# Layer 0 attention from the third batch on: weighted sums kept with features on partitions, even and odd heads joined by small transfers in place of transposes

## The chip, the cores and the metric

The kernel runs on one core of a Trainium2 chip. The metric is device time in microseconds (us) of one execution. Inputs and outputs lie in HBM, and the whole two-layer network is one launch.

## The reference, cut to what matters

`x` and `ctx` are 8 batches of 256 tokens by 256 features, in float32. Two layers follow one another; each adds a gated attention and a gated feed-forward part to `x`. Only the attention of layer 0 is touched by the change:

```python
def _L0_xattn_ref(Q, K, V, Wq, bq, Wk, bk, Wv, bv, Wo, bo):   # 16 heads of 16 features
    q, k, v = Q @ Wq + bq, K @ Wk + bk, V @ Wv + bv           # each to (B, 16, S, 16)
    scores = jnp.einsum('bhqd,bhkd->bhqk', q, k) * scale
    attn = jax.nn.softmax(scores, axis=-1)
    out = jnp.einsum('bhqk,bhkd->bhqd', attn, v)
    out = out.transpose(0, 2, 1, 3).reshape(B, S, D_MODEL)
    return out @ Wo + bo
x = x + jnp.tanh(g_xattn[0]) * _L0_xattn_ref(_layernorm(x), ctx_1024, ctx_1024, ...)
x = x + jnp.tanh(g_ffn[0]) * _L0_ffn_ref(_layernorm(x), ...)                  # 64 slots, top 8, GRU
x = x + jnp.tanh(g_xattn[1]) * _L1_xattn_ref(ctx_1024, _layernorm(x), ...)    # 8 heads of 128
x = x + jnp.tanh(g_ffn[1]) * _L1_ffn_ref(_layernorm(x), ...)                  # fake-quantized SwiGLU
```

## The kernel before, in words

**Tiles and engines.** A batch is one tile of 128 partitions x 2 x 256. TensorE (PE) does matmuls and 128x128 transposes into PSUM; PSUM has four banks tagged `m`, three tagged `z` and one tagged `s`. Batches 0 and 1 of layer 0 run first, together with the preparation of the weights. Batches 2 to 7 of layer 0 and the slot feed-forward of layer 0 then run beside the attention of layer 1 (`attention1`), which goes through 8 batches x 8 heads. The feed-forward of layer 1 comes last.

**What sets the order.** `layer0()` makes a list of pieces for each batch, each piece with a cost. The lists of batches 2 to 7 are joined with the pieces of the slot sets (`merge`) into the queue `side`. For each head of layer 1, `attention1` spends a share of credits on pieces of this queue, half after the softmax of the head and half at the end of the step. The share is worked out from the costs that are left and from the heads at which a batch must be ready. Below that, a tile scheduler decides the order on each engine by when an instruction is ready in its own planning; each engine then runs strictly in that order, and so does the queue of DMAs on SyncE (SP).

**Layer 0 attention of one batch.** Sixteen heads are taken in four groups `g` of four heads (`HG = 4`).

- `value` (L556 to L573): `ve` holds, for 128 keys and each head, 16 columns of values and 16 columns of ones. Two additions on VectorE (DVE, L568) write the values.
- `stack` (L593 to L611): for batches from 2 on, queries and keys were split into a high and a low half and stored to a DRAM scratch, and two transfers (L601) and four transfers (L605) on SP bring four heads of a group into the tiles `k` and `q` of one of two pairs.
- `scores`, `maxima`, `exps` (L613 to L653): the matmuls of L623, a negated maximum on DVE (L626), its transpose (L636), and the matmuls of L649 with the exponential on ScalarE (ACT, L652).
- `sums` (L655 to L675): eight matmuls (L660), four heads side by side: rows 32j to 32j+15 of the bank are the weighted values of head j by feature, rows 32j+16 to 32j+31 are sixteen equal copies of its sum of exponentials. ACT copies the bank to `oS` (L675).
- `divide` (L677 to L692): two transposes of `oS` (L682) put tokens on partitions, DVE takes the reciprocal of the eight sums of a token (L685) and multiplies (L687) into `o`.
- `turn_o` (L694): when all four groups are done, four transposes (L272, called from `turned`) bring `o` back to features on partitions, and ACT copies them to `oT` (L696).
- `finish` (L698 to L710): four matmuls with `wo` (L703), and DVE adds the result to `x` with its gate (L710).

Layer 1's parts that appear below: `query` L1045 and L1054, `key` L1081 and L1088, `value` L1101 and L1108, scores L1124 with the maximum on DVE (L1125) and the exponential on ACT (L1126), L1127 and L1128 on DVE, `turn_e` L1138 with the copies L1142 (DVE) and L1144 (ACT), `sums` L1152, and the turn of the latents (L272, then L1035 on DVE).

In the trace a float32 matmul has two records, a transpose has one, and the matmuls of L623 and L649 have one.

Of the kernel before, what the change touches and what calls it, by code (L numbers as in the profile page):

```python
# [9 lines left out]
F32 = mybir.dt.float32  # L10
# [6 lines left out]
ALU = mybir.AluOpType  # L17
# [4 lines left out]
P = 128  # L22
B, S, D = 8, 256, 256
EPS = 1e-5
H0, DK0 = 16, 16
HG = 4
# [17 lines left out]
BASE, ZERO = 1024.0, 1152.0  # L44

WARM = (12, 8, 15, 9)

SLOT_SETS = ((0,), (1,), (2, 3), (4, 5), (6, 7))

# [51 lines left out]
def flamingo_kernel(ctx: ExitStack, tc: tile.TileContext, a: dict, out: bass.AP):  # L101
    nc = tc.nc
    V, A, G, T = nc.vector, nc.scalar, nc.gpsimd, nc.tensor
# [10 lines left out]
    def bank(tag, dtype=F32):  # L114
        return psum.tile([P, 512], dtype, tag=tag, name=f"bank_{tag}", bufs=BANKS[tag])
# [9 lines left out]
    def load_tokens(b, queue):  # L125
        queue.dma_start(out=xs[b], in_=x_in[b])
        queue.dma_start(out=cs[b], in_=c_in[b])

    def rows(pool, tag, ap, n, queue):

        t = pool.tile([P, n], F32, tag=tag, name=tag)
        queue.dma_start(out=t, in_=ap.partition_broadcast(P))
        return t
# [24 lines left out]
    at0 = right0.enter_context(tc.tile_pool(name="at0", bufs=2, side="right"))  # L158
# [16 lines left out]
    bv = rows(w0, "bv", a["L0_xattn_bv"], D, nc.sync)  # L175
# [293 lines left out]
    class Batch0:  # L469
# [86 lines left out]
        def value(self):  # L556
            pp = self.bank().rearrange("p (m t) -> p m t", m=2)
            for m in range(2):
                for c in range(2):
                    T.matmul(  # L560
                        pp[:, m, :],
                        self.cT[:, c, m * P : (m + 1) * P],
                        wv[:, c, :],
                        start=c == 0,
                        stop=c == 1,
                    )
            for m in range(2):
                V.tensor_tensor(  # L568
                    self.ve[:, m, :, :DK0],
                    pp[:, m, :].rearrange("p (h e) -> p h e", e=DK0),  # L570
                    bv.rearrange("p (h e) -> p h e", e=DK0),
                    ALU.add,
                )  # L573
# [19 lines left out]
        def stack(self, g):  # L593

            if self.b < 2:
                return self.spread(g)
            q, k = self.pairs[g % 2]
            at = slice(g * HG, (g + 1) * HG)
            for i in range(2):
                half = 2 * DK0 * i  # L600
                nc.sync.dma_start(  # L601
                    out=k[half : half + 2 * DK0, :, :].bitcast(F32), in_=self.dk[:, :, at, :]
                )
            for r in range(4):
                ins = nc.sync.dma_start(  # L605
                    out=q[r * DK0 : (r + 1) * DK0, :, :].bitcast(F32), in_=self.dq[r // 2][:, at, :]
                )
            for far in (1, 2):
                if g == far - 1 and (far == 2 or self.b == 2) and self.b + far < B:
                    with tc.issue_after(ins.ins):  # L610
                        load_tokens(self.b + far, nc.sync)  # L611
# [43 lines left out]
        def sums(self, g):  # L655

            po = self.bank()[:, :S]

            def product(kc, j):
                return T.matmul(  # L660
                    po[32 * j : 32 * j + 32, :],
                    self.ve[:, kc, g * HG + j, :],
                    self.e[j // 2][:, j % 2, kc, :],
                    start=kc == 0,
                    stop=kc == 1,
                ).ins


            with tc.issue_after(product(0, HG - 1)), tc.high_priority():
                for j in range(HG - 1):  # L670
                    product(0, j)
                for j in range(HG):
                    product(1, j)
            self.oS = self.pool.tile([P, S], F32, tag="oS", name="oS", bufs=1)
            A.copy(self.oS, po)  # L675

        def divide(self, g):  # L677
            if g == 0:
                self.o = self.tmp(name="o") if self.b == 0 else at0.tile([P, 2, D], F32, tag="o", name="o", bufs=1)
            pt = self.bank()[:, : 2 * P].rearrange("p (c t) -> p c t", c=2)  # L680
            for qc in range(2):
                T.transpose(pt[:, qc, :], self.oS[:, qc * P : (qc + 1) * P], ident)  # L682
            pv = pt.rearrange("p c (j e) -> p c j e", e=2 * DK0)
            rs = small.tile([P, 2, HG], F32, tag=f"rs0{self.s}", name="rs0")
            V.reciprocal(rs, pv[:, :, :, DK0])  # L685
            at = g * HG * DK0
            V.tensor_tensor(  # L687
                self.o[:, :, at : at + HG * DK0].rearrange("p c (h e) -> p c h e", e=DK0),
                pv[:, :, :, :DK0],
                rs[:, :, :, None].to_broadcast([P, 2, HG, DK0]),  # L690
                ALU.mult,
            )  # L692
# [19 lines left out]
    def layer0():  # L712


        bs = [Batch0(b) for b in range(B)]
        out = [[] for _ in range(B)]

        def piece(cost, obj, name, *args):
            return (cost, lambda: getattr(obj, name)(*args))

        def head(me, groups):
            return [
                piece(0.0, me, "norm"),
                piece(0.5, me, "turn_c"),
                piece(1.8, me, "key"),
                piece(0.5, me, "turn_x"),
                piece(1.8, me, "query"),
            ] + [piece(0.0, me, "stack", g) for g in groups]

        def maxima(me, g):  # L730
            return [piece(0.5, me, "scores", g, qc) for qc in range(2)] + [piece(0.1, me, "maxima", g)]

        for b in range(2):
            out[b] += head(bs[b], range(2)) + maxima(bs[b], 0)
        for b in range(B):
            me = bs[b]
            after = bs[b + 1] if 0 < b < B - 1 else None
            for g in range(NG):
                nxt = (me, g + 1) if g + 1 < NG else (after, 0)
                far = (me, g + 2) if g + 2 < NG else (after, g + 2 - NG)  # L740
                work = [piece(0.5, me, "exps", g, 0)]
                if nxt[0]:
                    work.append(piece(0.5, nxt[0], "scores", nxt[1], 0))
                work.append(piece(0.5, me, "exps", g, 1))
                if nxt[0]:
                    work.append(piece(0.5, nxt[0], "scores", nxt[1], 1))
                if g == 0:
                    work.append(piece(1.8, me, "value"))
                if after:
                    if g == 0:  # L750
                        work.append(piece(0.0, after, "norm"))
                    if g == 1:
                        work.append(piece(0.5, after, "turn_x"))
                        work.append(piece(0.5, after, "turn_c"))
                        work.append(piece(1.8, after, "query"))
                    if g == 2:
                        work.append(piece(1.8, after, "key"))
                if nxt[0]:
                    work.append(piece(0.1, nxt[0], "maxima", nxt[1]))
                work.append(piece(1.8, me, "sums", g))  # L760
                if far[0]:
                    work.append(piece(0.0, far[0], "stack", far[1]))
                work.append(piece(0.3, me, "divide", g))
                out[b] += work
        for b in range(B):
            out[b] += [piece(0.5, bs[b], "turn_o"), piece(1.8, bs[b], "finish")]
        return bs, out


# [209 lines left out]
    first = [go for _, go in work0[0][HEAD:]]  # L979
# [364 lines left out]
    def keep_busy(to, n):  # L1344

        w = ffn["hq"][:, B - 1, 0:2, :].rearrange("p i s -> p (i s)")
        for _ in range(n):
            T.matmul(to, w[:, :P], w, start=True, stop=True)

    def attention1():  # L1350
# [80 lines left out]
        with tc.issue_after(me.projected):  # L1431
            keep_busy(bank("s"), WARM[0])
        me.norm()
# [11 lines left out]
    def one():  # L1445
        return big()[:, :512]
# [6 lines left out]
    with (  # L1453
# [4 lines left out]
        for n in range(NB):  # L1458
            h = fk.tile([P, IC, 512], F32, tag=f"h{n}", name=f"h{n}")
# [34 lines left out]

        sx, rx = act_scale(amax, clip[:, 0:1], "x", WARM[1], final.late)
        A.copy(cs[B - 1], turned_in(one(), final.xl))
# [72 lines left out]
        with tc.issue_after(filled):  # L1569
            keep_busy(one(), WARM[2])  # L1570
        sh, rh = act_scale(hmax, clip[:, 1:2], "h", WARM[3])
        out_v = out.rearrange("b (t p) d -> b p t d", p=P)
# [39 lines left out]
        for b in range(B):  # L1612
# [11 lines left out]
            for at in (slice(0, 2),) if b < B - 1 else (slice(0, 1), slice(1, 2)):  # L1624
                n = at.stop - at.start
# [47 lines left out]
```

## Time and profile before

| | us |
|---|---|
| runs before: lowest, median, highest of 3 | 979.39, 979.61, 982.68 |
| the profiled execution's own time | 977.19 |
| its span | 975.4 |
| busy: PE, DVE, ACT, GpSimd (POOL) | 937.7, 616.3, 466.6, 140.1 |
| last oS copied, last matmul of `finish` begins | 621.3, 633.1 |

The span is the part of the execution between the first and the last instruction of the program; 1.8 us of the profiled execution lie around it. A page of the profile gives the busy time of each engine, the chain of work that ended last, and the costliest groups of instructions by line. Busy times of PE are unions of records that overlap, since matmuls are pipelined; the distance from one start to the next, or the time that the chain gives to a record, is what a matmul costs. "Waits" views tell which instruction waited for which, and the timeline gives single instructions in order of time.

### The profile page before, as it was taken

Reading aid. Unit: us, or ns where it says so; the run is one execution under the profiler, and the core shown is the slowest. Engines: PE = TensorE matmul, PEld = TensorE weight load, DVE = VectorE, ACT = ScalarE, POOL = GpSimd, SP = SyncE. Lnnn points to the kernel's source line nnn. Section 1 sums busy time; section 2 is a strip of 40 time slices with the busy share of each in tenths; the row PEclk is TensorE's granted clock in tenths of the full one; section 3 lists DMA queues with packets and bytes.
Section 4 is the critical chain, followed back from the end, with each engine's and each line's share of the span. In section 5 each row is a group of like instructions: output and inputs, shape, how many; then the busy total and the mean of one; then the engine's idle time right before and its main releaser. Section 6 shows DMA issues by size and latency. Waiting matters only on the chain.

```text
span 975.4 us, 13331 instructions
## 1 busy us (share of the span) xinstructions
PE 937.7 (96%) x4875; PEld 692.5 (71%) x4877; DVE 616.3 (63%) x1620; ACT 466.6 (48%) x924; POOL 140.1 (14%) x181
## 2 busy tenths in 40 slices
PE   5989999999999999999999999999999999999996
PEld 3767778877777777777777677676766776777744
DVE  7765777774656747655657655566965365354477
ACT  4786545553546434554544443443444234333494
POOL 7101210110110202101011000014100010000172
PEclk9999999999999999999999999999999999999999
DMA  6803201111211102120001000000200000000012
GB/s 147 250 2 95 80 22 44 58 51 44 77 33 44 45 3 63 44 65 23 22 23 44 23 23 22 1 1 5 85 1 1 1 1 0 1 1 1 1 33 87
DMA packets 35186, 38.13 MB, mean 39 GB/s; under 512 B 10480, under 2 KB 30640, under 8 KB 35120
## 3 DMA queue, kind: packets, MB, share of 16 engines
q1 hardware_dynamic: 33488, 36.48, 12.8%
q0 software_dynamic: 1632, 0.79, 0.5%
q8 instruction: 39, 0.64, 0.3%
q14 instruction: 27, 0.22, 0.1%
HBM read 28.08 MB, written 8.39 MB: 37 GB/s over the span
## 4 chain that ended last, share of the span: by engine, by line
PE 82%; DVE 9%; ACT 5%; issue 1%; DMA 1%; POOL 1%; SPq 1%; DVEq 0%; ACTq 0%; POOLq 0%
PE bank_m L1152 10%; PE bank_m L1101 10%; PE bank_m L1081 10%; PE bank_m L1124 9%; PE bank_m L1045 5%; PE bank_m L1138 5%; PE bank_m L1165 5%; PE bank_z L623 3%; PE bank_z L649 2%; PE bank_z L531 2%; PE bank_z L660 2%; PE bank_s L876 1%; PE bank_z L703 1%; PE bank_z L560 1%; PE bank_z L272 1%
## 5 line engine op out<-in xcount | busy, mean ns | idle before, releaser
L1126 ACT ACTIVATE e<-bank_m,nm 128x512 f32<-128x512 f32 x128 | 87.9, 687 | 143.7 <-DVE nm L1125 141.6
L1152 PE MATMUL bank_m<-eT,v 128*128 128x256 f32 x496 | 120.6, 381 | 1.1 <-ACT k L1088 0.8
L1081 PE MATMUL bank_m<-kvT,w1kv 128*128 128x512 f32 (+1 forms) x256 | 118.4, 575 | 0.8 <-ACT e L1126 0.8
L1152 PEld LDWEIGHTS bank_m<-eT,v 128*128 128x128 f32 x496 | 92.4, 190 | 32.3 <-issue 14.8
L1101 PE MATMUL bank_m<-w1kv,kvT 128*128 128x256 f32 x480 | 110.0, 379 | 0.0
L1124 PE MATMUL bank_m<-k,q 128*128 128x512 f32 x224 | 109.5, 594 | 0.0
L1125 DVE TENSOR_REDUCE nm<-bank_m 128x1 f32<-128x512 f32 x128 | 87.6, 686 | 27.6 <-PE bank_m L1124 23.6
L1101 PEld LDWEIGHTS bank_m<-w1kv,kvT 128*128 128x128 f32 x480 | 89.8, 190 | 11.5
L652 ACT ACTIVATE e<-bank_z 128x512 f32<-128x512 f32 x112 | 62.8, 597 | 73.4 <-PE bank_z L649 73.0
L1054 DVE TENSOR_SCALAR q<-bank_m,bq 128x256 f32<-128x256 f32 x64 | 27.9, 478 | 87.3 <-PE bank_m L1045 87.3
L255 POOL TENSOR_TENSOR rstd<-rstd,mhalf 128x2 f32<-128x2 f32 x48 | 35.6, 743 | 321.5 <-DVE rstd L254 273.3
L626 DVE TENSOR_REDUCE nf<-bank_z 128x2 f32<-128x512 f32 x112 | 74.2, 681 | 9.7 <-PE bank_z L623 9.4
L1108 DVE COPY v<-bank_m 128x512 f32<-128x512 f32 x62 | 42.5, 686 | 55.2 <-PE bank_m L1101 55.2
L1138 PEld LDWEIGHTS bank_m<-ident,e 128*128 128x128 f32 x512 | 59.7, 141 | 23.1 <-issue 16.5
L1138 PE MATMUL bank_m<-ident,e 128*128 128x128 f32 x512 | 71.7, 274 | 0.8 <-DVE q L1054 0.5
L1159 ACT ACTIVATE oT<-bank_m,bv 128x256 f32<-128x256 f32 x64 | 30.3, 473 | 80.9 <-PE bank_m L1152 80.9
L1088 ACT ACTIVATE k<-bank_m,bk 128x512 f32<-128x512 f32 (+1 forms) x64 | 42.4, 662 | 47.7 <-PE bank_m L1081 47.2
L1045 PE MATMUL bank_m<-kvT,w1q 128*128 128x256 f32 x256 | 62.7, 381 | 1.7 <-DVE kvT L1035 1.6
L1128 DVE TENSOR_SCALAR e<-e,rs 128x512 f32<-128x512 f32 x128 | 62.1, 485 | 2.2
L1081 PEld LDWEIGHTS bank_m<-kvT,w1kv 128*128 128x128 f32 x256 | 43.3, 190 | 26.2 <-issue 22.1
L1165 PE MATMUL bank_m<-w1o,oT 128*128 128x256 f32 x256 | 60.1, 380 | 0.2 <-DVE x L1179 0.2
L1045 PEld LDWEIGHTS bank_m<-kvT,w1q 128*128 128x128 f32 x256 | 47.9, 190 | 11.0 <-DVE kvT L1035 2.2
(383 smaller groups left out, 1613.0 us busy)
## 6 DMA issues: line engine op xcount, KB each, us to landing
qs<-dqb SPq DMA_DIRECT2D x96, 64.0 KB, 2.6
ks<-dkb SPq DMA_DIRECT2D x48, 128.0 KB, 2.8
c<-in_ctx_dram SPq DMA_DIRECT2D x8, 256.0 KB, 3.1
x<-in_x_dram SPq DMA_DIRECT2D x8, 256.0 KB, 2.9
w1kv<-in_L_xattn_Wkv_dram SPq DMA_DIRECT2D x4, 512.0 KB, 6.5
out_dram<-y SPq DMA_DIRECT2D x7, 256.0 KB, 3.6
dqb<-hi SPq DMA_DIRECT2D x6, 256.0 KB, 2.2
dqb<-lo SPq DMA_DIRECT2D x6, 256.0 KB, 2.2
```

What stands on the lines that cost most here:

```text
L626: V.tensor_reduce(full[:, 2 * half : 2 * half + 2], ps, AX.X, ALU.max, negate=True)
L652: A.activation(e[:, i, :, :], ps, AF.Exp)
L1045: T.matmul(pq[:, i, :], w1q[:, c, h * P : (h + 1) * P], self.kvT[:, c, S:], start=c == 0, stop=c == 1,)
L1081: T.matmul(pk[:, at], w1kv[:, c, h * P : (h + 1) * P], self.kvT[:, c, at], start=c == 0, stop=c == 1,)
L1101: T.matmul(pv[:, k, :], (self.mT, self.kvT[:, :, S:])[half][:, c, k * P : (k + 1) * P], w1kv[:, c, at : at + 2 * P], start=c == 0, stop=c ...
L1124: T.matmul(ps, q, self.k[h], start=True, stop=True)
L1125: V.tensor_reduce(nm[:, at], ps, AX.X, ALU.max, negate=True)
L1126: A.activation(e[:, qc, :], ps, AF.Exp, bias=nm[:, at], accum_out=sums[:, at])
L1128: V.tensor_scalar(e[:, qc, :], e[:, qc, :], rs[:, at], None, ALU.mult)
L1138: T.transpose(pt[:, k, qc * P : (qc + 1) * P], self.e[h][:, qc, kc * P : (kc + 1) * P], ident)
L1152: T.matmul(po, self.v[h // 2][kc // 2][:, kc % 2, (h % 2) * P : (h % 2 + 1) * P], self.eT[:, kc, :], start=kc == 0, stop=kc == 3,)
L1165: self.projected = T.matmul(self.pp[:, qc, :], self.oT[:, h, qc * P : (qc + 1) * P], w1o[:, h, :], start=h == 0, stop=h == H1 - 1,).ins
```

## The change

For batches 2 to 7, `divide` and `turn_o` are no longer made. A group now takes every second head of eight: group 0 the even heads of the first eight, group 1 the odd ones, and groups 2 and 3 likewise of the second eight; the transfers of `stack` and the weights in `sums` step over the heads accordingly. For odd heads `ve` holds the ones first and the values behind them (a memset on POOL once, in batch 2; DVE writes the values in four additions instead of two). With that, the rows of features of an even group lie where the rows of sums of the odd group lie, and the reverse. ACT copies the bank of an even group straight into its half of `oT`, that of an odd group into `oS`. Transfers of 16 rows x 256 (16 KB each), issued on SP by `move`, take the sums of the even group to `rs` (four), the sums of the odd group to `rs` (four) and the features of the odd group into `oT` (four). DVE takes the reciprocal of the whole of `rs` (128x256), and POOL multiplies `oT` by it. `finish` of batches 2 to 6 is put behind the first five pieces of the next batch (`LEAD = 5`).

```diff
+LEAD = 5
...
         def value(self):
+            if self.b == 2:
+                G.memset(self.ve.rearrange("p m (h s) f -> p m h s f", s=2)[:, :, :, 1, :DK0], 1.0)
             for m in range(2):
+                if self.b > 1:
+
+                    ve, pv, bias = (
+                        x.rearrange("p (h s e) -> p h s e", s=2, e=n)
+                        for x, n in (
+                            (self.ve[:, m, :, :].rearrange("p h f -> p (h f)"), 2 * DK0),
+                            (pp[:, m, :], DK0),
+                            (bv, DK0),
+                        )
+                    )
+                    for i in range(2):
+                        V.tensor_tensor(
+                            ve[:, :, i, i * DK0 : (i + 1) * DK0], pv[:, :, i, :], bias[:, :, i, :], ALU.add
+                        )
+                    continue
...
         def stack(self, g):
-            at = slice(g * HG, (g + 1) * HG)
+            at = slice(g // 2 * 2 * HG + g % 2, (g // 2 + 1) * 2 * HG, 2)
...
         def sums(self, g):
             po = self.bank()[:, :S]
+            first, step = (g * HG, 1) if self.b < 2 else (g // 2 * 2 * HG + g % 2, 2)
...
-                    self.ve[:, kc, g * HG + j, :],
+                    self.ve[:, kc, first + step * j, :],
...
+            if self.b > 1 and g == 0:
+                self.oT = at0.tile([P, 2, S], F32, tag="o", name="oT", bufs=1)
+            if self.b > 1 and g % 2 == 0:
+                o = self.oT[:, g // 2, :]
+                A.copy(o, po)
+                self.sums_of = self.tmp(name="rs")[:, 0, :]
+                return self.move(self.sums_of, 0, o, 1)
             self.oS = self.pool.tile([P, S], F32, tag="oS", name="oS", bufs=1)
             A.copy(self.oS, po)
+            if self.b > 1:
+
+                o = self.oT[:, g // 2, :]
+                self.move(self.sums_of, 1, self.oS, 0)
+                self.move(o, 1, self.oS, 1)
+                V.reciprocal(self.sums_of, self.sums_of)
+                G.tensor_tensor(o, o, self.sums_of, ALU.mult)
+
+        def move(self, dst, to, src, which):
+
+            for j in range(HG):
+                a, b = ((2 * j + i) * DK0 for i in (to, which))
+                nc.sync.dma_start(out=dst[a : a + DK0, :], in_=src[b : b + DK0, :])
...
-                work.append(piece(0.3, me, "divide", g))
+                if b < 2:
+                    work.append(piece(0.3, me, "divide", g))
                 out[b] += work
         for b in range(B):
-            out[b] += [piece(0.5, bs[b], "turn_o"), piece(1.8, bs[b], "finish")]
+            if b < 2:
+                out[b].append(piece(0.5, bs[b], "turn_o"))
+            elif b < B - 1:
+
+                out[b], out[b + 1] = out[b] + out[b + 1][:LEAD], out[b + 1][LEAD:]
+            out[b].append(piece(1.8, bs[b], "finish"))
```

## The prediction, made before the changed kernel ran

> **What bounds the kernel now.** I read the page's busy line first, then the busy time by stage, then the chain that ended last.
>
> ```profile
> PE 937.7 (96%) x4875; PEld 692.5 (71%) x4877; DVE 616.3 (63%) x1620; ACT 466.6 (48%) x924; POOL 140.1 (14%) x181
> ```
> ```profile
> 118.00:640.00 522.00, 516.53 (x2790) 389.85 (x2790) 336.81 (x935) 248.02 (x501) 61.54 (x79) 1.00 0.12 36
> 640.00:875.00 235.00, 232.11 (x1009) 167.56 (x1008) 138.26 (x339) 91.14 (x192) 19.88 (x23) 1.00 0.03 10
> ```
> The columns after the stretch and its length are PE, PEld, DVE, ACT and POOL, then granted clock, DMA share and GB/s. The edited batches lie in the first stretch. PE is busy for 516.5 of its 522 us and for 232.1 of the 235 us of layer 1 alone behind it, at a granted clock of 1.00. So a microsecond taken from PE there is not eaten by another engine's bound, unless that engine's order makes PE wait. DVE is the next, with 336.8 of 522 us (65%).
>
> ```profile
> 616.76 0.22 PE bank_z L682 x2
> ...
> 625.73 3.46 PE bank_m L1101 x16
> 629.19 0.22 PE bank_z L682 x2
> 629.40 0.22 PE bank_z L272 x2
> ```
> In the chain (start, us, what) the two transposes of L682 take 0.22 us, so 0.11 us each; L1101 has two records for each matmul, so a 128x256 matmul takes 3.46 / 8 = 0.43 us. Adding the PE order of the kernel before up with such prices puts the last `finish` at 630 us, where the trace has 633.1: the order on PE, priced so, is the clock of this kernel.
>
> **PE: what is removed.** In batches 2 to 7, `divide` has 6 x 4 x 2 = 48 transposes and `turn_o` 6 x 4 = 24: 72 x 0.109 us (the median distance between starts) = 7.9 us, on the path. No matmul is added. The order of the changed kernel's instructions shows the rest of PE's work unchanged, in another interleaving; layer 0 gets ahead of layer 1, so the stage of layer 1 alone grows. It is as full (232.1 of 235), so I cost that at nothing; if that cover were gone, its idle share (1.2%) on 20 more us is 0.2 us.
>
> **ACT and POOL.** ACT loses six copies of L696 (0.585 us each): 3.5 us, off the path. POOL gains twelve products of 128x256 (0.74 us by L276): 8.9 us on an engine at 14%. Each product waits for its transfers and holds what is behind it; in the new order those are `lo` (L501), `rstd` (L255) and bias additions that wait for later DVE work anyhow. Nothing, except in the last batch (below).
>
> **SP.** 6 x 24 = 144 transfers are added.
>
> ```profile
> 304.06 1.81 SPq L605 DMA_DIRECT2D qs<-dqb  x4
> ```
> ```profile
> qs<-dqb SPq DMA_DIRECT2D x96, 64.0 KB, 2.6
> ```
> Four transfers of 16 rows issue in 1.81 us, 0.46 each, and land 2.6 us after issue (2.0 to 3.9). With the sums' matmuls over at T, ACT's copy is done by T+0.8 (620.9 to 621.6 in the trace); the four transfers of sums issue to T+2.2 and land at T+4.8; the last of eight issues at T+4.0 and lands at T+6.6. The loads of `stack` that stand behind them on SP come up to 3.7 us later. Against the new PE order, group by group, the tightest still lands about 1 us before its scores (batch 2, group 3: last load T+8.5, scores T+9.4). So nothing; bounds 0 to 3 us, if landings are at the long end. The loads now take 1 KB steps instead of 4 KB; stores of 1 KB rows (dqb<-hi, 256 KB) land in 2.2 us, so I cost that at nothing.
>
> **DVE.** It loses 24 x (0.198 L685 + 0.289 L687) = 11.7 us and has 24 additions of 128x128 (0.29) for 12 of 128x256 (0.41): +2.0 us. It gains twelve reciprocals of 128x256, a size that the trace does not show.
>
> ```profile
> L1127 DVE RECIPROCAL rs<-sum x128: 130/157/165, 133.0 to 910.1; 128x1 f32<-128x1 f32 x128
> ```
> ```profile
> L1230 DVE RECIPROCAL wrec<-wg_s x1: 191/191/191, 687.6 to 687.6; 128x6 f32<-128x6 f32 x1
> ...
> L1230 DVE RECIPROCAL wrec<-wds x1: 157/157/157, 693.3 to 693.3; 128x2 f32<-128x2 f32 x1
> ```
> ```profile
> L685 DVE RECIPROCAL rs<-bank_z x28: 186/197/208, 66.4 to 629.9; 128x8 f32<-128x8 f32 x28
> ```
> Below, the cost is that of any other 128x256 operation: 0.41 us (L260). Above, it grows by element as these rows do: one element 0.157, six 0.184 and 0.191, so 6.1 ns for each more, and 0.157 + 255 x 0.0061 = 1.71 us. I take 1.71, since the slope is of reciprocals and the 0.41 is not. DVE's sum is then -11.7 + 2.0 + 20.5 = +10.8 us, to 347.6 of 522: it does not become the bound.
>
> [...]
>
> **The new wait.** Every reciprocal stands in DVE's queue behind four landings (T+4.8). What matters is what DVE has behind it. I placed each of the twelve by the new DVE and PE orders.
>
> - The worst is batch 4, group 3. DVE is free at about T+1.2, waits to T+4.8, works to T+6.5, then makes two statistics (0.75) and turns `kvT` (L1035, 0.48): T+7.7. PE wants it for L1045 at T+5.0; without the reciprocal it would be ready at T+5.7. Loss 2.1 us.
> - Likewise: batch 2, group 3, `eT` (L1142) for L1152, 1.0; batch 3, group 3, a bank held until a maximum (L1125) is done, 0.8; batch 4, group 1, a z bank that L626 frees, 1.5; batch 5, group 3, `eT`, 0.9; batch 6, group 3, `eT`, 1.4.
> - In the other six what is behind comes later than T+6.5 in any case (mostly `q` of L1054): 0.
> - In the last batch POOL's product ends at T+6.6+0.75 = T+7.4, and the last three matmuls of `finish` stand at T+6.5: 0.9 us. Five other `finish` stand 14 us or more behind.
>
> The six places sum to 7.7 us. Half of that is my value, since the trace has DVE held without harm to PE:
>
> ```profile
> 625.77 0.73 DVE L260 TENSOR_SCALAR ln<-x,mv,rstd 128x256 f32<-128x256 f32 x2 [3.04 <-PE bank_m L272]
> ...
> 628.61 0.73 DVE L260 TENSOR_SCALAR ln<-ln,mv,rstd 128x256 f32<-128x256 f32 x2 [0.22 <-POOL rstd L255]
> ```
> For 3.6 us DVE serves one normalization here while PE runs through L1101. But the chain gives 9% of the span to DVE, so the cover is thin. Bounds: 0 (all hidden) and 12 x 1.71 = 20.5 us (every reciprocal on the path).
>
> **Sum.** -7.9 + 3.9 + 0.9 = -3.1 us. On the profiled execution: 977.19 - 3.1 = 974.1. The runs' median is 2.4 us above that execution, so on the runs: 979.61 - 3.1 = 976.5 us. Within 0.5% means 974.7 to 984.5; that is about what a measurement of this kernel can tell from no change.
>
> **Rivals.**
>
> - *All is hidden.* The reciprocal is short or always covered, and the whole 7.9 us stay: 971.7. For it: PE's waits for DVE are under 2 us in the whole first stretch before, and DVE loses 24 small pairs. Against it: the six places.
> - *Slower: the reciprocal at the head of DVE's queue.* DVE waits for landings in order, then holds 1.7 us or more, and maxima, `eT` and z banks are late each time. It decides from a loss of 7.9 / 12 = 0.66 us for each reciprocal; at 1.2 us it gives 979.61 - 7.9 + 14.4 = 986, with the whole 1.71 on PE 992. For it: DVE's 9% of the chain, slopes of the small reciprocals. Against it: the six groups with nothing urgent behind.
> - *It does not do what it says.* The transposes go, but PE waits in their place for the same results of ACT and DVE: 979.6. Against it: PE's waits add up to few us before.
>
> **How the numbers follow.** Forecast 0.42 (own range 972.5 to 980.5), all hidden 0.30, slower 0.18, no effect 0.10. Faster by over 0.5%: 0.10 of the forecast's and 0.27 of the hidden case's = 0.37. Slower by over 0.5%: 0.13 of the slower case. The rest, 0.50, is within. The range, 969.5 to 987, takes in all hidden with 2 us to spare and the slower case to 1.2 us each.
>
> **What would show it.** Right: no row for the 48 and 24 transposes, PE busy less by 7 to 8 us, RECIPROCAL 128x256 near 1.7 us, waits of PE for DVE up by some 4 us with `kvT` and `eT` named, a wait of the last batch's `finish` (L744 in the changed kernel) for POOL near 1 us. Wrong: a reciprocal of 0.4 us (then all hidden), scores waiting for `qs` or `ks` landings (then SP's queue was under-costed), or DVE idle for the transfers far over 4 us at a time (landings mis-sized).

## The result, and the profile after

The changed kernel takes 982.70 us (median of 22 runs, 978.38 to 987.10); the kernel before took 979.50 beside it (22 runs). The ratio is 1.0027, with a 95% interval of 1.0016 to 1.0038. So the change made the kernel 3.2 us slower by medians, where 3.1 us less were forecast. The difference is within the 0.5% that the prediction named, but its interval leaves out 1; as a sum of terms the forecast was 6.3 us off, and it had the wrong sign.

The profiled execution of the changed kernel took 984.52 us (span 982.7), 7.3 us more than the one of before. Not all of that is the change: the mean granted clock was 0.987 in this execution and 0.995 in the other. Over the changed kernel's 22 runs the mean is 0.991, over the 23 runs of the kernel before that were measured beside the first experiments 0.992. Within the runs of the kernel before, 0.001 of mean clock goes with 0.55 to 0.74 us, so between these medians the clock explains little. Between 150 and 900 us, past the windows of lower clock at the beginning (mean up to 130 us: 0.91 in the changed kernel, 0.97 before; from 150 to 900 us 1.00 in both), the same matmuls of the changed kernel fall about 2.4 us behind those of the kernel before in the two profiled executions. From here on, times of runs are compared with the kernel before measured beside them, and traces are used for places and waits.

The busy line of the page, and the busy time by stage (the columns are those explained in the prediction):

```profile
PE 936.3 (95%) x4803; PEld 690.6 (70%) x4805; DVE 634.5 (65%) x1596; ACT 463.8 (47%) x918; POOL 149.0 (15%) x194
```
```profile
118.00:640.00 522.00, 509.30 (x2710) 383.44 (x2709) 351.84 (x913) 242.66 (x490) 72.20 (x94) 0.99 0.14 41
640.00:875.00 235.00, 230.47 (x1004) 166.89 (x1003) 138.94 (x338) 90.94 (x192) 19.95 (x23) 1.00 0.03 10
```

PE has 72 records fewer (4875 to 4803), which are the transposes. DVE works 15.0 us more in the first stretch. That stretch is cut at the same 522 us in both, so the 7.2 us by which PE is busy less there (516.53 to 509.30) are not the transposes: they are idle time, 12.7 us where it was 5.5. In bare_lead4 below, which has the same transposes gone and none of the new work, PE is busy for 514.73 us of it.

The rows of the new work: the whole-tile reciprocal, then the transfers (KB each, median us from issue to landing):

```profile
L709 DVE RECIPROCAL rs<-rs x12: 1741/1752/1754, 176.0 to 624.3; 128x256 f32<-128x256 f32 x12
its engine sat idle before it (us, times) until:
  DMA rs<-oS: 16.5, 5
```
```profile
rs<-oT SPq DMA_DIRECT2D x48, 16.0 KB, 1.8
rs<-oS SPq DMA_DIRECT2D x48, 16.0 KB, 1.8
oT<-oS SPq DMA_DIRECT2D x48, 16.0 KB, 1.8
```

The reciprocal takes 1.752 us, against 1.71 worked out from the slope of the small ones. DVE stands idle for landings ahead of five of the twelve, 16.5 us in all. A transfer takes SP 0.59 us (0.46 was taken from the loads of `qs`) and lands 1.8 us after issue (2.6 taken).

The waits of PE from 118 to 640 us of the changed kernel (us in total, times, longest):

```profile
PE bank_m L1199 <- DVE eT L1189: 2.9, 2, 1.6
PE bank_m L1199 <- DVE rs L1174: 1.6, 1, 1.6
PE bank_z L744 <- POOL oT L710: 1.2, 1, 1.2
...
PE bank_z L669 <- DVE nf L646: 0.8, 1, 0.8
```

L1199 is the sums of layer 1 (L1152 before), and `eT` the copy that it needs. Before, all waits of PE for DVE in this stretch were 1.6 us:

```profile
PE bank_m L1045 <- DVE kvT L1035: 0.8, 3, 0.4
...
PE bank_m L272 <- DVE ln L260: 0.5, 1, 0.5
PE bank_m L1152 <- DVE nmb L630: 0.3, 1, 0.3
```

Now they are 7.1. The last `finish` (L744) waits for POOL's product.

### The profile page after: what moved, and what is told of

Its sections match the earlier page's. It is cut to its first block, busy times and chain, and to the rows that moved or that the text cites. A ratio compares the mean times of both kernels' runs of the same rounds, so it can differ in the third digit from the quotient of the medians.

```text
span 982.7 us, 13428 instructions
## 1 busy us (share of the span) xinstructions
PE 936.3 (95%) x4803; PEld 690.6 (70%) x4805; DVE 634.5 (65%) x1596; ACT 463.8 (47%) x918; POOL 149.0 (15%) x194
## 4 chain that ended last, share of the span: by engine, by line
PE 78%; DVE 10%; ACT 5%; DMA 4%; issue 2%; SPq 1%; POOL 1%; DVEq 0%; ACTq 0%; POOLq 0%
PE bank_m L1199 10%; PE bank_m L1148 10%; PE bank_m L1128 10%; PE bank_m L1171 9%; PE bank_m L1212 5%; PE bank_m L1092 5%; PE bank_m L1185 5%; PE bank_z L643 3%; PE bank_z L669 3%; PE bank_z L681 2%; PE bank_z L533 2%; PE bank_z L562 1%; PE bank_z L744 1%; PE bank_s L923 1%; PE bank_m L274 1%
## 5 line engine op out<-in xcount | busy, mean ns | idle before, releaser
L1199 PE MATMUL bank_m<-eT,v 128*128 128x256 f32 x496 | 120.1, 381 | 5.4 <-DVE eT L1189 2.9
L1199 PEld LDWEIGHTS bank_m<-eT,v 128*128 128x128 f32 x496 | 92.4, 190 | 37.6 <-issue 13.2
L1171 PEld LDWEIGHTS bank_m<-k,q 128*128 128x128 f32 x224 | 40.5, 190 | 24.5 <-issue 21.4
```

What stands on the lines that cost most here:

```text
L1171: T.matmul(ps, q, self.k[h], start=True, stop=True)
L1199: T.matmul(po, self.v[h // 2][kc // 2][:, kc % 2, (h % 2) * P : (h % 2 + 1) * P], self.eT[:, kc, :], start=kc == 0, stop=kc == 3,)
```

## The experiments

The table gives each kernel's median, that of the kernel before measured beside it, their difference, and the ratio with its 95% interval. The ratio is not formed from the two medians; it can differ from theirs by 1 to 1.5 us, and differences of that size are not to be read.

| kernel | what is different from the changed kernel | us | before | diff. | ratio |
|---|---|---|---|---|---|
| changed | | 982.70 | 979.50 | +3.2 | 1.0027 (1.0016 to 1.0038) |
| e4_bare | no transfers, reciprocals, products | 973.85 | 979.86 | -6.0 | 0.9948 (0.9932 to 0.9964) |
| e5_moves | no reciprocals, products | 977.44 | 980.51 | -3.1 | 0.9976 (0.9963 to 0.9989) |
| e6_product | no reciprocals | 977.46 | 980.51 | -3.1 | 0.9975 (0.9958 to 0.9991) |
| e1_narrow | reciprocal of 16 columns | 978.75 | 979.86 | -1.1 | 0.9989 (0.9975 to 1.0003) |
| e2_nowait | reciprocal of `oS`, no wait for transfers | 981.06 | 979.86 | +1.2 | 1.0011 (0.9996 to 1.0026) |
| e7_double | two reciprocals | 993.91 | 980.51 | +13.4 | 1.0142 (1.0108 to 1.0176) |
| e11_short | its order, 16 columns | 978.58 | 979.83 | -1.3 | 0.9989 (0.9969 to 1.0008) |
| e10_long | order of e1_narrow, 256 columns | 984.22 | 979.83 | +4.4 | 1.0049 (1.0025 to 1.0072) |
| e12_lead0 | LEAD = 0 | 998.09 | 979.83 | +18.3 | 1.0190 (1.0153 to 1.0227) |
| bare_lead4, bare_lead7 | e4_bare, LEAD = 4, 7 | 971.12, 971.88 | 979.77 | -8.7, -7.9 | 0.9907 (0.9883 to 0.9930), 0.9919 (0.9894 to 0.9944) |
| moves_lead4, moves_lead7 | e5_moves, LEAD = 4, 7 | 979.23, 980.97 | 979.77 | -0.5, +1.2 | 0.9986 (0.9967 to 1.0005), 1.0004 (0.9986 to 1.0023) |
| pool_lead4 | moves_lead4, transfers on POOL | 970.50 | 980.25 | -9.8 | 0.9916 (0.9888 to 0.9944) |
| e3_poolpow | reciprocal on POOL | 1359.07 | 979.86 | +379 | 1.3882 (1.3850 to 1.3913) |
| e9_compact | reciprocal of 128x16 | 976.25 | 980.51 | -4.3 | 0.9961 (0.9944 to 0.9979) |
| e13_twoqueues | e9, last batch on two queues | 972.90 | 979.83 | -6.9 | 0.9930 (0.9905 to 0.9955) |
| pool_compact | e13, LEAD = 4, features on POOL | 975.70 | 980.25 | -4.6 | 0.9949 (0.9931 to 0.9968) |

The theory at the start was that the transposes are saved, and that DVE, held in order by the wait for landings and by the long reciprocal, gives the gain back through late `eT`, `kvT` and banks. The rivals: a lower clock early in the execution, the 144 transfers in SP's queue, and the other planned order.

The medians are not corrected for the granted clock, whose mean over a kernel's runs lies between 0.988 and 0.992 here, but for e7_double (0.986), e12_lead0 (0.985) and e3_poolpow (0.858). Where 'between 150 and 900 us' stands below, the starts of the same matmuls in two traces are compared, past the windows of lower clock at the beginning; each is one execution, and where the orders differ it is good to some 0.5 us.

### Length, wait, transfers: four kernels

**e1_narrow.** The reciprocal is cut to 16 columns.

```diff
-                V.reciprocal(self.sums_of, self.sums_of)
+                V.reciprocal(self.sums_of[:, :16], self.sums_of[:, :16])
```

> The reciprocal covers 16 of the 256 columns of rs; the other 240 columns are left undivided. Its wait for the landed sums stays, its length on DVE goes from 1.75 us to about 0.25 (0.157 + 15 x 0.0061). Theory, the held DVE queue: each of the places where PE now waits for eT, kvT or a bank behind a reciprocal gets up to 1.5 us earlier, so the time falls by 5 to 8 us from the changed kernel's 982.7, to 975 to 978. If it is the waiting for landings ahead of the reciprocal and not its length: 980 to 982. Rival, early clock (the granted clock is below 1 in more windows ahead of 130 us): 982 to 984, nothing moves. Rival, SP's queue with 144 more transfers: 982 to 984 too.

Measured: -1.1 beside before, so 4.3 us better than the changed kernel, a little less than the theory expected. The rival of the early clock falls: by it a shorter reciprocal would have gained nothing.

**e2_nowait.** The reciprocal stays long but is taken from `oS`, into a tile that nobody reads.

```diff
-                V.reciprocal(self.sums_of, self.sums_of)
+                V.reciprocal(self.tmp(name="rs")[:, 0, :], self.oS)
```

> The reciprocal, still 128x256 and 1.75 us, is taken from oS, which ACT has copied at T+0.8, into a tile that nobody reads; the product takes the undivided sums, so the division is left out. DVE waits for no transfer any more, the transfers and POOL's product stay. Theory, held queue: DVE's 1.75 us stay but come some 4 us earlier; the wait's part goes: 977 to 981. If the length alone counts: 982 to 983. Rivals, early clock and SP's queue: 982 to 984.

Measured: +1.2, so 2.0 us better than the changed kernel, just above what was expected; the intervals of the two ratios overlap. It does not price the wait. DVE waits for no landing any more, but it still sits idle for 13.2 us ahead of the reciprocals, 9.6 of them for ACT's copy to `oS`, where the changed kernel has 16.5.

**e3_poolpow.** The reciprocal is a power on POOL.

```diff
-                V.reciprocal(self.sums_of, self.sums_of)
+                G.tensor_tensor(self.sums_of, self.sums_of, minus1.to_broadcast([P, S]), ALU.pow)
```

> The reciprocal is made on POOL as a power of minus one (a tensor-tensor power with a broadcast column), so DVE neither waits for the transfers nor works; the result is kept. Theory, held queue: every place is freed, and the time falls to 971 to 976, plus what the power is longer than a product in the last batch (a 128x2 power takes 0.70 us, a 128x256 product 0.73; if the power grows by element as the reciprocal does, some 2 us more there). Rivals, early clock and SP's queue: 982 to 984, or higher by a slow power.

Measured: 1359.07 us, a plain miss. The row of the power on POOL:

```profile
L711 POOL TENSOR_TENSOR rs<-rs,minus x12: 41126/41137/41285, 170.2 to 955.0; 128x256 f32<-128x256 f32 x12
```

One power of 128x256 takes 41.1 us, so this version says nothing about DVE.

**e4_bare.** Transfers, reciprocals and products are gone.

```diff
-                self.sums_of = self.tmp(name="rs")[:, 0, :]
-                return self.move(self.sums_of, 0, o, 1)
+                return
...
-                self.move(self.sums_of, 1, self.oS, 0)
-                self.move(o, 1, self.oS, 1)
-                V.reciprocal(self.sums_of, self.sums_of)
-                G.tensor_tensor(o, o, self.sums_of, ALU.mult)
```

> The transfers, the reciprocals and POOL's products are left out: finish multiplies undivided sums, with odd heads wrong. What is left of the change is the missing transposes, the other order of the heads in the loads, the four additions and the other order of pieces. This is the ceiling: theory, 979.5 - 7.9 = 971 to 973. Rival, early clock: 976 to 980, since the extra loss of clock stays. Rival, the loads in 1 KB steps or the other order of pieces: 977 or more.

Measured: -6.0, at 973.85 somewhat above the expected 971 to 973. The gain is there without the new work, and 4.9 us lie between this kernel and the narrow reciprocal. The theory of DVE alone does not explain those.

### Each part of the new work by itself

**e5_moves** leaves out the reciprocals and the products, **e6_product** the reciprocals alone, **e7_double** has two reciprocals.

```diff
-                V.reciprocal(self.sums_of, self.sums_of)
-                G.tensor_tensor(o, o, self.sums_of, ALU.mult)
```
```diff
-                V.reciprocal(self.sums_of, self.sums_of)
```
```diff
+                V.reciprocal(self.sums_of, self.sums_of)
```

> The reciprocals and POOL's products are left out, the 144 transfers stay, but nothing on an engine waits for the sums that they bring. Against the bare kernel (973.85) this prices the transfers and SP's queue alone. If the transfers are hidden: 973 to 975, with finish of the last batch waiting for the last landing. If the 4.9 us between the narrow reciprocal and the bare kernel lie in SP's queue: 977 to 979.

> Only the reciprocals are left out: the product takes undivided sums, DVE does nothing and waits for nothing. Against the kernel with transfers alone this prices POOL's products, above all in the last batch, where PE waited 1.2 to 1.6 us for them: 1 to 2 us more than e5_moves. Against the narrow reciprocal (978.75) it prices DVE's waiting for the landings without its length: if waiting costs what taking the reciprocal from oS gave back (1.5 us), 977; if all of the 4.9 us is waiting, 974.

> Two reciprocals of 128x256, one behind the other, so the sums are undivided again: 3.5 us of DVE behind each wait in place of 1.75. From 16 to 256 columns 1.5 us more on each of twelve cost 3.8 us (0.32 us each), a fifth of the added DVE time. If that share holds, 1.75 us more cost 4.4 us: 987. Theory, held queue: the cover of the small places is used up, so more than that: 988 to 998, at most 982.7 + 21 = 1004. If the planned order and not the length made the difference between the narrow and the full reciprocal: 981 to 985.

e5_moves and e6_product are both 3.1 us better than before, where 1 to 2 us between them were expected. By medians the products cost nothing; in the traces PE waits 1.3 us for them in the last `finish`, against 0.5 for a landing in e5_moves, and between 150 and 900 us e6_product loses 1.0 us against e5_moves. The mean clock of e5_moves' runs is the lower one (0.988, 0.990), which is enough to hide that. The transfers take back 2.9 us of the bare kernel's 6.0; the intervals of these two ratios just touch. From e6_product (-3.1) to e1_narrow (-1.1), whose matmuls stand in the same order, DVE's wait for the landings and 0.25 us of work cost 2 us; the intervals of the two ratios overlap, so this one is not firm. Between 150 and 900 us e1_narrow loses 2.1 us, but 1.5 of them at 342 to 345 us, where it runs at half clock behind a pause of 1.6 us that e6_product has too. The double reciprocal costs 10.2 us more than the single one, half of the 21 us that DVE works more, and more than the 4.4 us of an even share. The cover being used up, as the theory of the held queue said, agrees with this; the other planned order and the lower clock of its runs were not taken apart from it.

### Length against planned order

A shorter instruction also changes the plan: about a tenth of PE's matmuls stand elsewhere in e1_narrow. So two kernels cross length and order. The instruction is changed after the planning, with every list and every wait of the engines left as planned: **e11_short** runs the changed kernel's order with 16 columns, **e10_long** the narrow kernel's order with all 256.

```diff
+    for f in nc.m.functions:
+        for block in f.blocks:
+            for i, ins in enumerate(block.instructions):
+                if type(ins).__name__ == "InstReciprocal" and list(ins.outs[0].ap[1]) == [1, 256] and "rs_" in ins.outs[0].memref:
+                    block.instructions[i] = _copy.replace(
+                        ins, outs=[cut(p, 16) for p in ins.outs], ins=[cut(p, 16) for p in ins.ins]
+                    )
```

(e10_long has 16 and 256 the other way round, on e1_narrow; `cut` sets the number of columns.)

> The order of the changed kernel, with the twelve reciprocals cut to 16 columns after the planning; 240 columns are left undivided. Theory, length: 982.7 - 4 = 977 to 980. If the planned order made the difference: 981.5 to 983.5.

> The order of the narrow kernel (planned with a reciprocal of 16 columns), with the instruction itself widened to all 256 columns after the planning; the result is kept. Every engine runs the list of the narrow kernel; only the twelve reciprocals are longer, 1.75 us in place of 0.25. Theory, the length of the held DVE queue: 978.75 + 4 = 982 to 986 (above the changed kernel's 982.7, since its own plan knew the long instruction). If the planned order made the difference: 978 to 980.

| | 16 columns | 256 columns |
|---|---|---|
| order of the narrow kernel | -1.1 | +4.4 |
| order of the changed kernel | -1.3 | +3.2 |

The length costs 5.5 us in one order and 4.5 in the other, and in neither do the intervals of the two ratios overlap; the order alone costs 0.2 and 1.2, less than the intervals. The length it is. The traces say the same: between 150 and 900 us the changed kernel loses 4.4 us against e11_short, both at full granted clock there (1.00 in the changed kernel; e11_short has 0.996 over its whole execution), and e10_long 6.6 us against e1_narrow, each with one window of 3.4 us at half clock. One place, in the same order, batch 5, group 3, by DVE's timeline (start, us, what, idle before and its cause) in the changed kernel and in e11_short:

```profile
444.41 0.69 DVE L1172 TENSOR_REDUCE nm<-bank_m 128x1 f32<-128x512 f32 x1 [0.17 <-PE bank_m L1171]
446.30 1.75 DVE L709 RECIPROCAL rs<-rs 128x256 f32<-128x256 f32 x1 [1.20 <-DMA rs<-oS]
447.97 0.10 DVE L1174 RECIPROCAL rs<-sum 128x1 f32<-128x1 f32 x1
447.99 0.67 DVE L1172 TENSOR_REDUCE nm<-bank_m 128x1 f32<-128x512 f32 x1
448.58 0.68 DVE L1175 TENSOR_SCALAR e<-e,rs 128x512 f32<-128x512 f32 x1
449.18 0.68 DVE L1189 COPY eT<-bank_m 128x512 f32<-128x512 f32 x1
```
```profile
439.20 0.69 DVE L1172 TENSOR_REDUCE nm<-bank_m 128x1 f32<-128x512 f32 x1 [0.17 <-PE bank_m L1171]
440.76 0.25 DVE L709 RECIPROCAL rs<-rs 128x16 f32<-128x16 f32 x1 [0.87 <-DMA rs<-oS]
...
441.94 0.68 DVE L1189 COPY eT<-bank_m 128x512 f32<-128x512 f32 x1
```

And PE in the same two kernels, at the matmul that needs `eT`:

```profile
447.79 0.60 PE L274 MATMUL bank_s<-ident,xn 128*128 128x128 f32 x4
450.00 1.32 PE L1199 MATMUL bank_m<-eT,v 128*128 128x256 f32 x5 [1.61 <-DVE rs L1174]
```
```profile
442.58 0.60 PE L274 MATMUL bank_s<-ident,xn 128*128 128x128 f32 x4
443.01 1.89 PE L1199 MATMUL bank_m<-eT,v 128*128 128x256 f32 x8
```

With the long reciprocal `eT` begins 4.77 us after the maximum of the first line, with the short one 2.74. PE's wait of 1.61 us is there in the one and gone in the other. The wait for the landing ahead of it (1.20 and 0.87) is in both.

### LEAD

**e12_lead0** puts `finish` back to the end of its own batch.

```diff
-LEAD = 5
+LEAD = 0
```

> LEAD = 0: finish of batches 3 to 7 of 8 stands at the end of its own batch again, right behind the last group's pieces. The product is ready some 7 us after the sums' matmuls, so finish waits: the last batch loses 1.2 us in that place. Five more such places at 1 to 5 us: 985 to 1000. If other pieces fill the place in the planned order: 982 to 985.

Measured: +18.3, 15 us worse than LEAD = 5. Without the distance PE waits for POOL's product in four of the `finish` pieces' places (3.6 us in all), and for `eT` and `kvT` 3.6 and 3.2 us. Between 150 and 900 us the loss against the kernel before is 16.2 us, and it has two windows at half clock, 10.2 us long together; the rest was not taken apart. The prediction costed the five early `finish` at nothing because they stand 14 us behind; with LEAD = 0 they do not.

### The transfers

The 2.9 us of the transfers were left: only one wait of PE for a landing shows in e5_moves (0.5 us, the last `finish`), but its planned order differs from the bare kernel's in about a tenth of the matmuls. Two other values of LEAD give other orders to both.

```diff
-LEAD = 5
+LEAD = 4
```
```diff
-LEAD = 5
+LEAD = 7
```

> The bare kernel (no transfers, reciprocals, products) with finish one piece earlier, which gives PE another order: 416 of its 3515 matmuls stand elsewhere. If the order is worth little: 972.5 to 975, as with LEAD = 5 (973.85). If the missing 1.9 us of the 7.9 lie in that one order: 970 to 972, or as far on the other side.

> The kernel with transfers alone, with finish one piece earlier. If the 3 us belong to the transfers: 2 to 4 us above the bare kernel with the same LEAD. If they belong to the order: 0.5 to 1 us above it (the last finish waits 0.6 us for a landing), or any other distance.

> The bare kernel with finish two pieces later; 646 matmuls stand elsewhere. As for LEAD = 4: 972.5 to 975 if the order is worth little.

> The kernel with transfers alone, with finish two pieces later. As for LEAD = 4: 2 to 4 us above the bare kernel of the same LEAD if the transfers cost it, 0.5 to 1 or any other distance if the order does.

The bare kernel gains 8.7 and 7.9 us (6.0 with LEAD = 5). The transfers cost 2.9, 8.1 and 9.1 us; with LEAD = 4 and 7 the intervals lie far apart. They cost time in every order, so it is not the chance of one. Between 150 and 900 us they cost 3.2, 6.0 and 9.6 us; the 9.6 hold one window of 6.8 us at half clock. So some 2 us of the 8.1 may be the lower clock at the beginning.

The queue of transfers on SP (start, us, what), first in bare_lead4, then in moves_lead4, shows how. It is the same group's loads in both:

```profile
206.48 0.80 SPq L621 DMA_DIRECT2D ks<-dkb  x2
207.33 1.89 SPq L625 DMA_DIRECT2D qs<-dqb  x4
```
```profile
215.71 0.80 SPq L621 DMA_DIRECT2D ks<-dkb  x2
216.55 1.37 SPq L625 DMA_DIRECT2D qs<-dqb  x3
222.54 2.41 SPq L714 DMA_DIRECT2D rs<-oT  x4
224.99 0.58 SPq L625 DMA_DIRECT2D qs<-dqb  x1
```

In the bare kernel the six loads of the group go out together. In the other one the group before is already some 9 us later, 3.5 of them by the clock at the beginning; the first five go out 9 us later, and the last stands behind four transfers that wait for ACT's copy of the sums, and goes out 16 us later. The first scores of that group come at 217.42 in the one and at 228.75 in the other. Over the 24 groups, the last load lands less than 2.5 us ahead of the first scores in 2 groups of bare_lead4, 10 of moves_lead4 and 9 of the changed kernel, against 3 in the kernel before (the trace has the landings of about half of the loads, and of none in one group of each kernel with transfers on SP). The issues are all there: the last load is issued less than 5 us ahead of the first scores in 5 groups of bare_lead4, 14 of moves_lead4 and 14 of the changed kernel, against 4 in the kernel before. PE shows no wait there: the plan already puts the scores later. What is late is layer 0 as a whole, and a wait can show where layer 1 takes it over. The longest of PE's waits in moves_lead7 (200 to 640 us):

```profile
PE bank_m L274 <- DVE ln L262: 2.9, 1, 2.9
```

That is the turn of the next batch's latents, which need layer 0 finished. The bare kernel with the same LEAD has no such wait.

**pool_lead4** moves the 144 transfers to POOL's queue. Its matmuls then stand as in bare_lead4 but for 3.

```diff
-                nc.sync.dma_start(out=dst[a : a + DK0, :], in_=src[b : b + DK0, :])
+                nc.gpsimd.dma_start(out=dst[a : a + DK0, :], in_=src[b : b + DK0, :])
```

> The kernel with transfers alone and LEAD = 4, with all 144 transfers issued by POOL in place of SP. The planned order is then that of the bare kernel with LEAD = 4 but for 3 of 3515 matmuls, where SP's transfers move 349. If what the transfers cost (8 us in this pair) comes from their place in SP's queue, through the order planned around it: 971 to 973, near the bare kernel's 971.12, with at most 0.6 us for the last landing. If the transfers themselves cost it, by their traffic and landings: 977 to 979.5.

Measured: -9.8, as good as the bare kernel (ratios 0.9916 and 0.9907); two groups, as in bare_lead4, have their loads less than 2.5 us ahead. The loads of the group shown above go out together again:

```profile
213.88 0.80 SPq L621 DMA_DIRECT2D ks<-dkb  x2
214.74 2.03 SPq L625 DMA_DIRECT2D qs<-dqb  x4
```

The profiled execution of this kernel is the longest of its six runs (977.36 us, clock 0.984). It lies 8.4 us behind that of bare_lead4 (clock 0.996) at 150 us already, by windows of lower clock, and 8.1 us behind at 900 us. So the traffic and the landings of the transfers cost nothing that shows. Their place in SP's queue, ahead of loads that did not need to wait, costs all of it, with LEAD = 4; the changed kernel with its transfers on POOL's queue was not run.

### Versions that keep the result

**e9_compact.** One row of sums of each head goes through a DRAM scratch into 128x16, the reciprocal is taken there, and a second scratch spreads it again. The last batch stays as it was.

```diff
+                    nc.sync.dma_start(out=few, in_=self.sums_in.rearrange("k (i t) -> (k i) t", t=DK0))
+                    self.move(o, 1, self.oS, 1)
+                    V.reciprocal(few, few)
...
+                    nc.sync.dma_start(
+                        out=self.sums_of, in_=back[:, None, :].to_broadcast([2 * HG, DK0, S])
+                    )
```

> A version that keeps the result. In batches 3 to 7 of 8 one row of sums of each head goes through a DRAM scratch into 128x16, DVE takes the reciprocal of 128x16 (about 0.25 us), and a second scratch brings it back as 16 rows for each head; the last batch stays as in the changed kernel, since nothing covers two more landings there. Theory, held queue: like the narrow reciprocal or better (978.75), since the wait for the two hops can be planned behind other work: 975 to 979. If the longer way makes finish late: 980 to 985.

Measured: -4.3, better than the narrow reciprocal, at the good end of what was expected. The ten small reciprocals take 0.251 us each.

**e13_twoqueues.** In the last batch ACT issues the four transfers of sums of an odd group.

```diff
-                self.move(self.sums_of, 1, self.oS, 0)
+                self.move(self.sums_of, 1, self.oS, 0, nc.scalar)
```

> The compact version; in the last batch the four transfers of sums of an odd group are issued by ACT, beside the four of features on SP, so that all eight are issued by T+3.2 rather than T+5.8 and the product ends some 1 to 2 us sooner. PE's wait of 1.0 us for it in the last finish goes: 976.25 - 1 = 974.5 to 976. If ACT's issuing holds its exponentials: 976 to 978. The result is kept.

Measured: 972.90 us, -6.9, better than expected; the ratio 0.9930 (0.9905 to 0.9955) makes it the fastest kernel here that keeps the result. PE's wait in the last `finish` fell only from 1.0 to 0.7 us, so the step from e9_compact is larger than its reason; its interval overlaps that of e9_compact, and why it gained more is open.

**pool_compact.** The features and the first store of sums go by POOL's queue, with LEAD = 4.

```diff
-                    self.move(o, 1, self.oS, 1)
+                    self.move(o, 1, self.oS, 1, nc.gpsimd)
```

> The compact version that keeps the result, with ACT issuing the last batch's sums, LEAD = 4, and the transfers of features and the first store of sums issued by POOL; 46 of 3515 matmuls stand elsewhere than in the bare kernel with LEAD = 4. If SP's queue is what the transfers cost: 971 to 973, against 972.9 with SP and LEAD = 5. If not: 973 to 977, since POOL's waits for the copies hold its other work.

Measured: -4.6, not the 971 to 973 that were expected, and not better than e13_twoqueues. What helps the transfers alone does not add up with the compact way; why is open (its other transfers stay on SP).

## Why the prediction was wrong

By differences to the kernel before, with LEAD = 5: the transposes and what went with them -6.0, the transfers +2.9, the products 0, the wait for landings with the first 16 columns +2.0, the other 240 columns +4.3; together +3.2, the measured difference (they add up because each is the step to the next kernel). The prediction's sum was -7.9 + 0 + 0 + 3.9 + 0.9. Of the 6.3 us between the two, 2.9 are the transfers on SP, 2.4 DVE and 1.9 the transposes' step, less 0.9 for the product. Between 150 and 900 us of the traces the same steps are -7.4, +3.2, +1.0, +2.1 and +3.5, together +2.4: there the transposes and the product are as predicted, the transfers and DVE are not.

- **Transposes, -7.9: right.** The 72 records are gone, and the bare kernels gain 6.0, 8.7 and 7.9, on average 7.5. Between 150 and 900 us the three gain 7.4, 7.4 and 7.3, so the 6.0 at LEAD = 5 is not a worse planned order. The prediction's sign, PE busy less by 7 to 8 us, is met in the first stretch by idle time alone; over the whole execution PE is busy 1.4 us less (937.7 to 936.3), part of it at half clock (0.50 within 51 to 59, 72 to 80 and 123 to 131 us).
- **SP, "So nothing; bounds 0 to 3 us": the step that failed most.** The working went group by group "against the new PE order" and found the tightest load 1 us ahead of its scores. That was right on the chip as far as it went: no scores wait for a landing. But the new PE order had itself been planned around the late loads, so a small distance there was the price and not its absence. The transfers cost 2.9 us here, at the end of the stated bounds, and 8 to 9 at other values of LEAD. That they cost it by the queue is shown by pool_lead4, at LEAD = 4. The prediction's sign for an under-costed queue, scores that wait for landings, could not show it. The loads in 1 KB steps, costed at nothing, land after 2.5 and 2.7 us, where it was 2.6 and 2.8.
- **Reciprocals, "Half of that is my value": mis-sized.** The six places summed to 7.7 us, and half was taken, 3.9. Wait and length together cost 6.3 (2.0 + 4.3); the 4.3 are firm, the 2.0 are not. The length was right (1.752 us, 1.71 predicted), and so was the way in which it costs (`eT` begins 4.77 us after the maximum in the place shown, 2.74 with 16 columns). The 16 columns at 0.251 us and the 256 at 1.752 give 6.3 ns for each column more, against the 6.1 of the prediction's slope. The evidence for the half, DVE held for 3.6 us while PE ran on, was one place in which nothing urgent stood behind.
- **The six places.** From the changed kernel's trace to e11_short's, in the same order, PE's waits ahead of L1199, which needs `eT`, in batches 2, 5 and 6, group 3, fall from 1.3, 1.6 and 0.8 us to 0.6 and none. Those were named (1.0, 0.9, 1.4). At two others that were named, batch 3, group 3, and batch 4, group 1, no wait of PE goes away. The worst one named, `kvT` in batch 4, group 3, was wrong: there PE's wait for `eT` (1.6 us) is just as long with the short reciprocal, since the plan has put `eT` ahead of the reciprocal.
- **The last `finish`, 0.9: right in the trace** (a wait of 1.2 us, some 0.9 of it due to the product), though leaving the product out gained nothing that the medians show.
- **The landings** took 1.8 us, not 2.6, but SP needed 0.59 for each issue, not 0.46; on the way to the last landing the two nearly cancel.
- **The range** (969.5 to 987.0) and "within 0.5%", the likeliest of the three, held. The rival that ends on the other side, the reciprocal at the head of DVE's queue, named the larger part of the loss. No rival had SP's queue as the cause of a loss.

## What to carry to other kernels

When work moves to a queue that runs in order (on SP, in moves_lead4, a load of `qs` went out at 224.99 us, behind four transfers that waited for ACT's copy), ask what stands behind it there, and do not take the planned order of the changed kernel as proof that nothing is late: the planner has already paid by moving the consumers back. A way to see it is the distance between a load's issue and its use, compared with the kernel before; a way to test it is the same transfers on another queue. An operation whose time grows with its columns should be made as small as its data allows (16 copies of each sum were divided here; 0.251 us in place of 1.752).

## What the runs showed of the hardware

- A tensor-tensor power on POOL took 0.70 us for 128x2 and 41.1 us for 128x256, some 159 ns for each column more. In `rstd` it looks as cheap as a product (0.73 us for 128x256).
- Behind some pauses of PE the granted clock was half. In moves_lead7, behind its wait of 2.9 us (the 0.50 is the clock):

```profile
346.20:353.00 6.80, 6.16 (x14) 4.01 (x15) 1.24 (x2) 1.34 (x3) 0.69 (x1) 0.50 0.36 106
```

  PE runs at half clock for 6.8 us, where bare_lead7 shows 1.00 in the same window. Between 130 and 930 us, seven such windows of 3.4 or 6.8 us begin in all the profiles (that of the power on POOL aside); six begin within 2.1 us of the end of a pause of PE of 1.6 us or more. Five of these six pauses lasted 1.6 to 2.9 us, the sixth 4.2 (e7_double). The 23 other pauses of that size have none behind them (the one of 1.61 us in the changed kernel, at 450 us, is among them), and one window has no such pause ahead of it, so the pause alone does not decide; what does is not shown.
